# Picking key and value rows from a table on TensorE: one and a half tiles a step with the sums behind the last subtraction, against two tiles a step with x picked

## Chip, cores, metric

The kernel runs on one core of one Trainium2 chip. The metric is the device time of one execution in microseconds (us). The engines are TensorE (PE, with its weight loads as PEld), VectorE (DVE), ScalarE (ACT), GpSimd (POOL) and SyncE (SP), which here only issues transfers.

## What is computed

One layer of a graph network on 6250 nodes of 64 values and 206250 edges, sorted by destination:

```
Qh, Kh, Vh = x @ W.T + b            # [6250, 4 heads, 16]
Ee    = edge_attr @ We.T + be       # [206250, 4, 16]
score = exp(clip((Kh[src] * Qh[dst] / 4 * Ee).sum(-1), -5, 5))
msg   = Vh[src] * score
x     = layernorm(x + segment_sum(msg, dst))
```

`src` is random, `dst` is sorted, so a tile of 128 edges needs 128 scattered rows of K and V, but only a small window of neighbouring rows of Q and of the output.

## The kernel before

**Tiles and steps.** 206250 edges make 1612 tiles of 128; 8 tiles are a group (G), two groups a step. There are 105 steps: 97 of 16 tiles (the steps 0 to 96) and 8 of one group. The order on each engine is the order of the program (the schedule is written by hand); the framework adds the semaphores. Within one PSUM tensor it keeps accesses in order.

**Ahead of the loop** the program writes a table of K and V rows (`kv_tab`, 512 bytes a row) and one of Q rows in three bfloat16 parts to HBM. K and V of the first four groups are computed from gathered rows of x (32 gathers at line 219).

**K and V of a tile** come in one of two ways.

- *Gathered.* `gather_kv` issues one indirect DMA on GpSimd for each tile: 128 rows of `kv_tab` into one of five buffers of a step (`kvs`). `gather(s + 4)` stands in step s, behind `message(s)`.
- *Picked.* In the steps M0 = 4 to LAST = 94 the last two tiles of step s + 2 are not gathered but picked. The table of x is held in SBUF as three bfloat16 parts (`parts`, 50 blocks of 125 nodes, 64 columns a part). `sources` (ScalarE) and `sources_turned` (TensorE, into `from_b` in PSUM) spread the source numbers of a tile over the partitions; `hots` (VectorE, line 470) compares them with the block numbers and makes 25 one-hot matrices in one instruction; `picks` (TensorE, line 480) multiplies them with 25 blocks of the table, 192 columns each. Two `hots` and two `picks` make a tile. `picked`, `picked_turned` and `picked_kv` add the three parts, turn the rows and multiply them with the weights of K and V (lines 487 to 505).

**A step** does, on the critical engines: `queries` (one-hot rows times the window of Q, into PSUM `pq`), `products` (K times Q, times the edge term `pe`), `scores`, `message` (V times score, into `pq`), then three bfloat16 parts of the message (`msg3`): ScalarE copies the first part, TensorE subtracts it in PSUM with a negative identity (`minus`, line 593), ScalarE copies the second, and so on. `sums` (line 601) multiplies one-hot edges with the three parts, 192 columns a tile, into `pa`; `add` puts `pa` onto the accumulator. `spread` and `onehot_rows` make the one-hot rows of the next step: TensorE writes into the one room `pb`, ScalarE squares it out, and a second pass makes the one-hot.

**PSUM.** There are eight banks, and all are taken: `pb`, `pe` and `pq` two each, `pick` (the picked rows) one, `small` one. `small` is shared:

```
small = fixed.tile([P, 4 * P], F32, name="small")
col, from0, from1 = (small[:, i * C:(i + 1) * C].bitcast(BF16) for i in range(3))
score_all = small[:, 3 * C:3 * C + 2 * G * H]
pa = small[:, 4 * C:7 * C].rearrange("p (i c) -> p i c", i=3)
```

**The order around the change.** In step s TensorE gets: spread of the next step's first group, `sums(s - 1)`, the turns, spread of the second group, edges, 25 picks, the turned x rows, edges, and then picks and minus in turn, `queries(s + 1)`, picks. VectorE gets products, picked, scores, `add(s - 1)`, message, two `hots`, the one-hot edges of the next step, two `hots`, and then closing of finished rows and normalising.

Of the kernel before, what the change touches and what calls it, by code (L numbers as in the profile page):

```python
# [14 lines left out]
P = 128  # L15
# [25 lines left out]
TB = 8  # L41
M0 = 4
# [21 lines left out]
LAST = NS - 8 - 3  # L64


def picks_in(s):
    return M0 <= s <= LAST

# [22 lines left out]
def tile_gnn(ctx: ExitStack, tc: tile.TileContext, x, xT, wT, bias, beT, weT, eT, src, dst, dst_rows,  # L92
# [51 lines left out]
    wkv = consts.tile([P, 2, 2 * C], F32, name="wkv")  # L144
    bkv_p = consts.tile([3, G // 2, 2 * C], BF16, name="bkv_p")
    minus_b = consts.tile([P, P], BF16, name="minus_b")
# [26 lines left out]
    with tc.tile_pool(name="nodes", bufs=1) as nodes, \  # L173
# [29 lines left out]

        nc.vector.memset(wkv, 0.0)
# [34 lines left out]
        nc.vector.tensor_scalar(minus_b, ident, -1.0, None, op0=OP.mult)  # L239
# [4 lines left out]
        nc.vector.memset(ones_b, 1.0)  # L244

# [155 lines left out]
    with tc.If(rv == 0) as branch:  # L401

        with tc.tile_pool(name="work", bufs=2) as work, \
# [11 lines left out]
            parts = accp.tile([P, NB, 3, C], BF16, name="parts")  # L415
            nc.vector.memset(parts, 0.0)
            NX = N // NB
            x_v = x.rearrange("(p b) c -> p b c", p=NX)
            n_picks = LAST - M0 + 1
            src_f = accp.tile([P, n_picks, 2], F32, name="src_f")  # L420
            t0 = (M0 + 3) * 2 * G - 2
            for i in range(2):
                nc.vector.tensor_copy(src_f[:, :, i],
                                      src_i[:, t0 + i:t0 + i + 2 * G * (n_picks - 1) + 1:2 * G])
            pick = fixed.tile([P, 4 * P], F32, name="pick")
            rows3 = pick[:, :6 * C].rearrange("p (k i c) -> p k i c", k=2, i=3)
            HOT, FAR, X = {}, {}, {}
# [5 lines left out]
            def table_parts(b):  # L433

                n = min(TB, NB - b)
                raw = work.tile([P, TB, C], F32, name="raw", bufs=1)
                nc.sync.dma_start(raw[:NX, :n], x_v[:, b:b + n, :])
                rest = pick[:NX, :n * C].rearrange("p (b c) -> p b c", b=n)
                nc.scalar.activation(rest, raw[:NX, :n], AF.Copy)
                nc.scalar.activation(parts[:NX, b:b + n, 0], raw[:NX, :n], AF.Copy)  # L440
                return rest

            def table_parts_rest(b, rest):
                n = min(TB, NB - b)
                nc.vector.tensor_sub(rest, rest, parts[:NX, b:b + n, 0])
                nc.scalar.activation(parts[:NX, b:b + n, 1], rest, AF.Copy)
                nc.vector.tensor_sub(parts[:NX, b:b + n, 2], rest, parts[:NX, b:b + n, 1])

            def sources(s, i):

                if picks_in(s):
                    FAR[s, i] = work.tile([P, P], BF16, name="far")
                    nc.scalar.activation(FAR[s, i], row50, AF.Identity,
                                         bias=src_f[:, s - M0, i:i + 1], scale=-1.0)

            def sources_turned(s, i):
                if picks_in(s):
                    nc.tensor.transpose(from_b[i], FAR.pop((s, i)), ident_b)  # L460

            def blocks(h):
                return slice(h * NB // 2, (h + 1) * NB // 2)

            def hots(s, i, h):

                if picks_in(s):
                    HOT[s, i, h] = work.tile([P, NB // 2, P], BF16, name="hot", bufs=4)
                    shape = [P, NB // 2, P // 2, 2]
                    nc.vector.tensor_tensor(  # L470
                        HOT[s, i, h].rearrange("p b (a c) -> p b a c", c=2),
                        pairs(from_b[i])[:, None].to_broadcast(shape),
                        block2[:, blocks(h), None, :].to_broadcast(shape), op=OP.is_equal)

            def picks(s, i, h):
                if picks_in(s):
                    hot = HOT.pop((s, i, h))
                    for k in range(NB // 2):
                        b = h * NB // 2 + k
                        nc.tensor.matmul(rows3[:, i], hot[:, k, :], parts[:, b], start=b == 0,  # L480
                                         stop=b == NB - 1)

            def picked(s):

                if picks_in(s):
                    xp = work.tile([P, 2, C], F32, name="xp")
                    nc.vector.tensor_reduce(xp, rows3.rearrange("p k i c -> p k c i"), axis=AX.X,
                                            op=OP.add)
                    X[s] = xp

            def picked_turned(s):
                if picks_in(s):
                    room = psum.tile([P, G, P], F32, name="pb")
                    nc.tensor.transpose(room[:, 0, :], X[s].rearrange("p k c -> p (k c)"), ident)
                    xe = work.tile([P, P], F32, name="xe")
                    nc.scalar.activation(xe, room[:, 0, :], AF.Copy)
                    X[s] = xe, room[:, 4:6, :]

            def picked_kv(s):
                if picks_in(s):  # L500
                    xe, kv = X.pop(s)
                    nc.tensor.matmul(kv, ones_b, bkv_p[:, :2], start=True, stop=False,
                                     skip_group_check=True)
                    nc.tensor.matmul(kv, xe, wkv, start=False, stop=True, skip_group_check=True)  # L504
                    nc.scalar.activation(kvs[(s + 2) % KVB][:, 2 * G - 2:, :], kv, AF.Copy)

            def gather(s):
                for g in groups_of(s):
                    for j in range(tiles_of(g)):
                        if not picks_in(s - 2) or g == STEPS[s][0] or j < G - 2:  # L510
                            gather_kv(g, j)
# [25 lines left out]

            def onehot_rows_rest(g):
                n = tiles_of(g)
                nc.scalar.activation(TO[g][:, :n, :], TO[g][:, :n, :], AF.Relu, bias=one_p[:3 * W],  # L540
                                     scale=-1.0)
# [11 lines left out]
            def queries(s):  # L553
                PQ[s] = psum.tile([P, 2 * G, C], F32, name="pq")
                for g in groups_of(s):
                    for j in range(tiles_of(g)):

                        nc.tensor.matmul(PQ[s][:, (g - STEPS[s][0]) * G + j, :], TO[g][:, j, :], QW[g],  # L558
                                         start=j == 0, stop=j == tiles_of(g) - 1,
                                         skip_group_check=True)  # L560
# [27 lines left out]
            def minus(s, msg, i):  # L588

                n = tiles_in(s)  # L590
                for lo in range(0, n, G):
                    hi = min(n, lo + G)
                    nc.tensor.matmul(msg[:, lo:hi, :], minus_b, M3[s][:, lo:hi, i, :], start=False,  # L593
                                     stop=True, skip_group_check=True)
                nc.scalar.activation(M3[s][:, :n, i + 1, :], msg[:, :n, :], AF.Copy)  # L595
# [69 lines left out]
            for k, g in enumerate(groups_of(0)):  # L665
                onehot_rows(g, spread(g))
                onehot_rows_rest(g)
                edges(0, k)
            queries(0)
            onehot_edges(0)  # L670
            for s in range(NS):
# [4 lines left out]
                if s + 2 < NS:  # L676
                    for g in groups_of(s + 2):
                        fetch_queries(g)
                nexts = list(groups_of(s + 1)) if more else []
                if more:  # L680
                    onehot_rows(nexts[0], spread(nexts[0]))
                    onehot_rows_rest(nexts[0])
                if s:
                    sums(s - 1)
                sources_turned(s, 1)
                sources_turned(s + 1, 0)
                if nexts[1:]:
                    onehot_rows(nexts[1], spread(nexts[1]))
                making = [b for b in range(s * 2 * TB, (s + 1) * 2 * TB, TB) if b < NB]
                if making:  # L690
                    rest = table_parts(making[0])
                prod = products(s)
                picked(s - 1)
                if more:
                    edges(s + 1, 0)
                picks(s, 0, 0)
                score = scores(s, prod)
                if nexts[1:]:
                    onehot_rows_rest(nexts[1])
# [5 lines left out]
                picked_turned(s - 1)  # L705
                if nexts[1:]:
                    edges(s + 1, 1)
                minus(s, msg, 0)
                hots(s, 1, 0)
                picks(s, 0, 1)  # L710
                minus(s, msg, 1)
                picked_kv(s - 1)
                if not more:

                    close(B - 2)
                    spreads(B - 2)
                hots(s, 1, 1)
                picks(s, 1, 0)
                sources(s + 1, 1)
                sources(s + 2, 0)  # L720
                if more:
# [3 lines left out]
                    queries(s + 1)  # L725
                picks(s, 1, 1)
                hots(s + 1, 0, 0)
                hots(s + 1, 0, 1)
# [19 lines left out]
            sums(NS - 1)  # L748
# [173 lines left out]
```

## Time and profile before

| | |
|---|---|
| time, median of 3 runs | 1808.15 us (1807.94 to 1808.39) |
| the profiled execution | 1808.39 us, its span 1806.6 us |
| busy: PE, PEld, DVE | 1641.5 us (91%), 1370.4 (76%), 1481.7 (82%) |
| busy: ACT, POOL | 912.0 us (50%), 1351.8 (75%) |
| mean granted TensorE clock | 0.95 of full speed |
| transfers | 166.30 MB, mean 92 GB/s |
| gathers of K and V | 1398, and 32 of x |

Busy times count what an engine executes; the issue of an indirect DMA is work of GpSimd and the time between two of them is shown as idle with the releaser "issue". Matmuls overlap in the records (a matmul's time includes its way through the array), so a stream of them is read from start to start. A releaser is inferred from semaphore events; for a wait on several it is the one that came last.

### The profile page before, as it was taken

The numbers are of one execution on the slowest core, as the hardware profiler recorded it, in microseconds if no ns is written. First come the engines' busy times: TensorE is split into PE (matmuls) and PEld (weight loads), VectorE is DVE, ScalarE is ACT, GpSimd is POOL, SyncE is SP. The second block draws the span as 40 slices with busy tenths as digits, with TensorE's granted clock in tenths as the row PEclk, the third lists the DMA queues.
The fourth block names the chain that finished last, engine by engine and source line by source line (L and its number), as shares of the span: only waits on it lengthen the run. The fifth ranks groups of instructions, "written<-read, shape, count | busy, mean of one in ns | idle before, by whom it ended". The sixth has DMA issues, their size and how long they took to land.

```text
span 1806.6 us, 38129 instructions
## 1 busy us (share of the span) xinstructions
PE 1641.5 (91%) x15751; PEld 1370.4 (76%) x15751; DVE 1481.7 (82%) x1695; ACT 912.0 (50%) x1313; POOL 1351.8 (75%) x1442
## 2 busy tenths in 40 slices
PE   8979999999999998999899898989999999999864
PEld 8547888888877777777777787877777778777632
DVE  6459999999988898888888888888988888888554
ACT  4465555555545454544545444455444545445443
POOL 7777777777777777777777777777777777777774
PEclk9968999999999999999999999999999999999855
DMA  8343323333323333332333323323332332332331
GB/s 239 112 120 92 92 80 104 80 101 83 92 79 93 91 84 90 99 81 81 92 91 90 80 79 93 91 79 98 84 92 80 92 91 79 91 91 79 89 79 45
DMA packets 106532, 166.30 MB, mean 92 GB/s; under 512 B 67501, under 2 KB 67822, under 8 KB 106236
## 3 DMA queue, kind: packets, MB, share of 16 engines
q0 software_dynamic: 45760, 92.76, 19.6%
q1 hardware_dynamic: 60204, 70.01, 13.5%
q8 instruction: 125, 2.05, 0.5%
q10 hardware_dynamic: 384, 1.00, 0.3%
q14 instruction: 59, 0.48, 0.1%
HBM read 156.32 MB, written 7.33 MB: 91 GB/s over the span
## 4 chain that ended last, share of the span: by engine, by line
PE 31%; POOL 28%; DVE 19%; issue 14%; DMA 4%; ACT 3%; DVEq 0%; SPq 0%; POOLq 0%; ACTq 0%
POOL kv L391 28%; PE pick L480 15%; DVE hot L470 7%; PE pe L380 4%; DMA kv<-kv_tab,src_i 4%; PE pq L593 2%; DVE prod L565 2%; DVE prod L566 2%; PE small L601 2%; DVE pq L582 2%; DVE small L572 2%; PE pb L518 2%; DVE acc L615 1%; PE pb L504 1%; PE pe L377 1%
## 5 line engine op out<-in xcount | busy, mean ns | idle before, releaser
L391 POOL DMA_INDIRECT kv<-kv_tab,src_i x1398 | 1319.7, 944 | 426.1 <-issue 403.5
L480 PE MATMUL pick<-parts,hot 128*128 128x192 bf16 x9100 | 825.6, 249 | 0.0
L480 PEld LDWEIGHTS <-hot 128*128 128x128 bf16 x9100 | 769.6, 99 | 38.0
L470 DVE TENSOR_TENSOR hot<-small,block 128x3200 bf16<-128x3200 bf16 x364 | 645.9, 1816 | 0.8 <-PE pick L480 0.8
L535 ACT ACTIVATE to<-pb,minus_row 126x1024 bf16<-126x1024 f32 x202 | 222.8, 1103 | 372.7 <-PE pb L518 368.7
L380 PEld LDWEIGHTS pe<-we_sb,et 128*128 128x128 f32 x1612 | 213.2, 206 | 152.9 <-issue 136.8
L595 ACT ACTIVATE msg<-pq 128x1024 bf16<-128x1024 f32 (+2 forms) x210 | 207.8, 990 | 219.7 <-PE pq L593 219.7
L565 DVE TENSOR_TENSOR prod<-kv,pq 128x1024 f32<-128x1024 f32 (+2 forms) x105 | 123.6, 1177 | 191.7 <-DMA kv<-kv_tab,src_i 92.7
L380 PE MATMUL pe<-we_sb,et 128*128 128x128 f32 x1612 | 254.3, 305 | 0.0
L540 ACT ACTIVATE to<-to,one_p 126x1024 bf16<-126x1024 bf16 x202 | 230.6, 1142 | 3.5
L377 PE MATMUL pe<-be_p,ones_b 3*128 3x512 bf16 x202 | 80.0, 396 | 104.8 <-DVE prod L566 104.8
L601 PEld LDWEIGHTS <-of 128*128 128x128 bf16 x1612 | 145.1, 102 | 30.9 <-issue 7.8
L601 PE MATMUL small<-msg,of 128*128 128x192 bf16 x1612 | 161.5, 256 | 0.5 <-ACT msg L595 0.5
L593 PE MATMUL pq<-msg,minus_b 128*128 128x512 bf16 x404 | 128.1, 396 | 30.8 <-ACT msg L585 16.6
L585 ACT ACTIVATE msg<-pq 128x1024 bf16<-128x1024 f32 (+2 forms) x105 | 103.9, 990 | 96.9 <-DVE pq L582 96.9
L572 DVE TENSOR_REDUCE small<-prod 128x64 f32<-128x1024 f32 (+2 forms) x105 | 123.6, 1177 | 13.3 <-PE small L460 7.5
L518 PE MATMUL pb<-key_rows,ident_b 112*128 112x512 bf16 x403 | 127.7, 399 | 2.8 <-ACT to L535 2.8
L566 DVE TENSOR_TENSOR prod<-prod,pe 128x1024 f32<-128x1024 f32 (+2 forms) x105 | 123.6, 1177 | 3.6
L582 DVE TENSOR_TENSOR pq<-kv,small 128x1024 f32<-128x1024 f32 (+2 forms) x105 | 123.5, 1176 | 1.4 <-ACT small L575 1.4
L548 DVE TENSOR_TENSOR of<-small,key 128x2048 bf16<-128x2048 bf16 (+2 forms) x105 | 123.2, 1173 | 0.3
L575 ACT ACTIVATE small<-small 128x64 f32<-128x64 f32 (+2 forms) x105 | 21.7, 207 | 131.0 <-DVE small L574 130.5
L558 PEld LDWEIGHTS <-to 126*128 126x128 bf16 x1612 | 63.5, 101 | 25.1 <-issue 24.9
(128 smaller groups left out, 992.1 us busy)
## 6 DMA issues: line engine op xcount, KB each, us to landing
et<-in_eT SPq DMA_DIRECT2D x100, 512.0 KB
kv<-kv_tab,src_i POOLq DMA_INDIRECT x1398
qw<-q_tab SPq DMA_DIRECT2D x202, 15.8 KB
kv_tab<-kv_sb SPq DMA_DIRECT2D x5, 640.0 KB
q_tab<-q SPq DMA_DIRECT2D x5, 480.0 KB
acc<-in_x SPq DMA_DIRECT2D x48, 32.0 KB
out<-y SPq DMA_DIRECT2D x48, 32.0 KB
raw<-in_x SPq DMA_DIRECT2D x6, 250.0 KB
```

The costliest lines, as they stand in the source:

```text
L380: nc.tensor.matmul(pe[:, 2 * u:2 * u + 2, :], et[:, u, :], we_sb, start=False, stop=u == n // 2 - 1, skip_group_check=True)
L391: nc.gpsimd.indirect_dma_start(out=kv_of(g)[:, j, :], out_offset=None, in_=kv_tab[:, :], in_offset=bass.IndirectOffsetOnAxis(ap=src_i[:, t ...
L470: nc.vector.tensor_tensor(HOT[s, i, h].rearrange("p b (a c) -> p b a c", c=2), pairs(from_b[i])[:, None].to_broadcast(shape), block2[:, bl ...
L480: nc.tensor.matmul(rows3[:, i], hot[:, k, :], parts[:, b], start=b == 0, stop=b == NB - 1)
L518: nc.tensor.matmul(pb[:, b:b + 4, :], ident_b[:NR2, g // 2:g // 2 + 1].to_broadcast([NR2, P]), key_rows[:, g % 2, b * P:(b + 4) * P], star ...
L535: nc.scalar.activation(TO[g][:, :n, :], pb[:3 * W, :n, :], AF.Square, bias=minus_row3[:3 * W])
L540: nc.scalar.activation(TO[g][:, :n, :], TO[g][:, :n, :], AF.Relu, bias=one_p[:3 * W], scale=-1.0)
L565: nc.vector.tensor_mul(prod[:, :n, :], kvs[s % KVB][:, :n, :C], PQ[s][:, :n, :])
L566: nc.vector.tensor_mul(prod[:, :n, :], prod[:, :n, :], PE[s][:, :n, :])
L593: nc.tensor.matmul(msg[:, lo:hi, :], minus_b, M3[s][:, lo:hi, i, :], start=False, stop=True, skip_group_check=True)
L595: nc.scalar.activation(M3[s][:, :n, i + 1, :], msg[:, :n, :], AF.Copy)
L601: nc.tensor.matmul(PA[s], OH[s][:, j, :], M3[s][:, j], start=j == 0, stop=j == n - 1)
```

## The change

The table in SBUF holds K and V themselves (128 columns a part) and is read back from `kv_tab`; so a pick has 384 columns, and the turning of x and the multiplication with the weights are gone. Three tiles are picked in every two steps, from step 9 on (tiles of the steps 11 to 96): 43 x 3 = 129 tiles in place of 182. A step has three units of 25 blocks in place of four. The parts of the message are made by two subtractions on VectorE (`message_rest`, `message_last`) in place of `minus` on TensorE. `queries(s)` moves from the end of step s - 1 to the beginning of step s; both `spread` of the next step stand together behind it; the second pass of `onehot_rows` stands directly behind the first. `sums(s)` stands directly behind `message_last(s)`, ahead of the next `hots`. Core of the diff:

```diff
-TB = 8
-M0 = 4
+TB = 4
+T0 = 2
+M0 = 9
+UNITS = 3
+PICKED = [(s + 2 + d, i) for s in range(M0, NS, 2) for d, i in ((0, 0), (0, 1), (1, 0))
+          if s + 3 < NS and STEPS[s + 3][1] == 2]
...
-            parts = accp.tile([P, NB, 3, C], BF16, name="parts")
-            nc.vector.memset(parts, 0.0)
+            parts = accp.tile([P, NB, 3, 2 * C], BF16, name="parts")
...
-            rows3 = pick[:, :6 * C].rearrange("p (k i c) -> p k i c", k=2, i=3)
+            rows3 = pick[:, :3 * P].rearrange("p (i c) -> p i c", i=3)
...
+            def hots(u):
+                HOT[u] = work.tile([P, NB // 2, P], BF16, name="hot", bufs=3)
+                shape = [P, NB // 2, P // 2, 2]
+                bs = slice(u % 2 * NB // 2, (u % 2 + 1) * NB // 2)
+                nc.vector.tensor_tensor(HOT[u].rearrange("p b (a c) -> p b a c", c=2),
+                                        pairs(from_b[u // 2 % 2])[:, None].to_broadcast(shape),
+                                        block2[:, bs, None, :].to_broadcast(shape), op=OP.is_equal)
+            def picks(u):
+                for i in range(NB // 2):
+                    b = u % 2 * NB // 2 + i
+                    nc.tensor.matmul(rows3, HOT[u][:, i, :], parts[:, b], start=b == 0,
+                                     stop=b == NB - 1)
+            def picked(k):
+                step, back = PICKED[k]
+                nc.vector.tensor_reduce(kvs[step % KVB][:, 2 * G - 1 - back, :],
+                                        rows3.rearrange("p i c -> p c i"), axis=AX.X, op=OP.add)
...
-            def minus(s, msg, i):
...
+            def message_rest(s, msg):
                 n = tiles_in(s)
...
+                nc.vector.tensor_sub(msg[:, :n, :], msg[:, :n, :], M3[s][:, :n, 0, :])
+                nc.scalar.activation(M3[s][:, :n, 1, :], msg[:, :n, :], AF.Copy)
+            def message_last(s, msg):
+                n = tiles_in(s)
+                nc.vector.tensor_sub(M3[s][:, :n, 2, :], msg[:, :n, :], M3[s][:, :n, 1, :])
```

The loop of a step after the change, without the conditions of its ends (`u = (s - M0) * UNITS`; `picked_of(u)` acts for odd u, where a tile is complete):

```
fetch_edges, fetch_queries
queries(s)
for g in nexts:
    onehot_rows(g, spread(g))
for k in turning:
    sources_turned(k, FAR.pop(k))
if making:
    rest = table_parts(making[0])
picks_of(u)
prod = products(s)
edges(s + 1, 0)
picked_of(u)
picks_of(u + 1)
edges(s + 1, 1)
score = scores(s, prod)
add(s - 1)
msg = message(s, score)
gather(s + KVB - 1)
hot_of(u + 2)
picked_of(u + 1)
picks_of(u + 2)
message_rest(s, msg)
keys, onehot_edges(s + 1)
message_last(s, msg)
sums(s)
FAR[...] = sources(...)
hot_of(u + 3)
picked_of(u + 2)
hot_of(u + 4)
close, spreads, roots, scales, norm, table_parts_rest
```

## The prediction

> **What bounds the kernel now.** I read the page's groups first, then the start of every step (L565 opens a step on the Vector engine), one warm step in order of time, the waits, and the granted clock. The groups, with busy time and mean of one, then the idle time before them:
>
> ```profile
> L391 POOL DMA_INDIRECT kv<-kv_tab,src_i x1398 | 1319.7, 944 | 426.1 <-issue 403.5
> L480 PE MATMUL pick<-parts,hot 128*128 128x192 bf16 x9100 | 825.6, 249 | 0.0
> L470 DVE TENSOR_TENSOR hot<-small,block 128x3200 bf16<-128x3200 bf16 x364 | 645.9, 1816 | 0.8 <-PE pick L480 0.8
> ```
>
> GpSimd never stops: 944 ns for a gather and 0.30 us of issue behind it, so 1.2485 us apart. With the 32 gathers of L219 it makes 1430 from 2.94 us on, 1430 x 1.2485 + 2.9 = 1788 us; 18 us remain to the span's end, 1806.6. The starts of L565 agree: steps 6 to 25 take 31.4 us a pair, 15.7 each; from step 26 they take 17.4 to 17.5, which is 14 gathers x 1.2485 = 17.48, and L565 waits for gathered rows. So GpSimd sets the end, and TensorE could do a step in 15.7. That is seen in a warm step:
>
> ```profile
> 270.75 0.60 PE L518 MATMUL pb<-key_rows,ident_b 112*128 112x512 bf16 x2
> 271.18 1.48 PE L601 MATMUL small<-msg,of 128*128 128x192 bf16 x16
> 271.38 1.11 ACT L535 ACTIVATE to<-pb,minus_row 126x1024 bf16<-126x1024 f32 x1 [3.99 <-PE pb L518]
> 272.50 0.28 PE L460 MATMUL small<-ident_b,far 128*128 128x128 bf16 x2
> 272.61 0.60 PE L518 MATMUL pb<-key_rows,ident_b 112*128 112x512 bf16 x2
> 273.14 0.39 PE L377 MATMUL pe<-be_p,ones_b 3*128 3x512 bf16 x1
> 273.46 1.16 PE L380 MATMUL pe<-we_sb,et 128*128 128x128 f32 x8
> 274.45 2.23 PE L480 MATMUL pick<-parts,hot 128*128 128x192 bf16 x25
> 276.51 0.27 PE L494 MATMUL pb<-ident,xp 128*128 128x128 f32 x1
> ```
>
> From start to start: spread 0.43, sums 1.32 (16 of 82.6 ns), two turns 0.11, edges 1.31, 25 picks 2.06. The two spreads share one room in PSUM, so the second starts 1.86 us after the first, behind L535; the sums lie in that gap.
>
> **The gathers.** Picked tiles fall from 182 to 129 (43 x 3), so GpSimd makes 1451 + 32 = 1483 gathers: 53 more, 66 us. Floor: 2.9 + 1483 x 1.2485 + 18 = 1872 of span. In the picking steps it is 14.5 x 1.2485 = 18.1 a step. Nothing hides this; something slower may.
>
> **TensorE's work.** A pick gets 384 columns. Rows at the clock of that step: 64 columns 26.9 ns (L558, 16 in 0.43), 192 columns 82.6, 512 columns 215. The line from 192 to 512 gives 162 (bounds 161 and 165), 25 take 4.06. Per step: 3 x 4.06 = 12.18, edges 2.62, sums 1.32, queries 0.43, spreads 0.86, turns 0.08: 17.5. Gone are one of four batches of 25, the four minus matmuls (0.96) and L494, L502, L504 (0.93).
>
> **The spreads' gap.** Both spreads now stand together behind queries, with nothing between: 1.86 - 0.43 = 1.43 us idle in every step. That makes 18.9.
>
> **The sums ahead of the comparisons.** The sums, turned sources, the scores and the key column all lie in the one PSUM bank of "small". How the program orders that bank is seen in a short step:
>
> ```profile
> 1738.01 1.49 PE L601 MATMUL small<-msg,of 128*128 128x192 bf16 x8
> 1738.12 0.69 DVE L566 TENSOR_TENSOR prod<-prod,pe 128x512 f32<-128x512 f32 x1
> 1739.53 0.69 DVE L572 TENSOR_REDUCE small<-prod 128x32 f32<-128x512 f32 x1 [0.73 <-PE small L601]
> ```
>
> L572 writes columns 192 to 255, L601 columns 256 to 447, yet L572 starts 0.03 us after L601's last matmul. So a comparison (hots, reading small) that follows sums(s) in the program will wait for it on VectorE, and the next turns (writing small) for those comparisons. The trace shows this for a write behind a write; for a read behind a write I take it over. The Trainium skill, "PSUM — Partial Sum Buffer", section "PSUM bank collisions raise a hardware error", says the same of reads and speaks against this change: two engines may not touch one bank and quadrant together, whatever the columns, so semaphores must guard whole banks. By addresses alone the sum would be 1957, by the bank rule 2093.
>
> Time 0 is the start of the sums, which stand behind the third batch of picks on TensorE. VectorE's subtraction is done 1.2 us earlier, then VectorE stands: its next comparison starts at 1.51 (sums 1.48 to the last matmul's end, 0.03). Comparisons start 1.73 apart, the second takes 1.82; every other step a reduction of the pick (0.47, row L487) stands between. So TensorE's turns start at 1.51 + 1.73 + 1.82 + 0.06 = 5.12, or 5.59. TensorE itself got there at 1.32 + 0.43 + 1.86 + 0.43 = 4.04: another 1.08 or 1.55 us idle. Behind the waiting turn are queued the whole 14.8 us of picks and edges, which end the step: 5.12 + 0.06 + 14.8 = 19.98, or 5.59 + 0.11 + 14.8 = 20.50; mean **20.24**. In place of this chain a shorter one (18.9) or a longer one could stand, below.
>
> **VectorE.** Two subtractions of 1024 elements come in; nearest row L582, also 1024 with the output in PSUM, 1.22 us. One comparison of 1.82 goes. Its chain in a step: products 2.5 (L565, L566), scores and exp 1.76 (L572 1.25, L574 0.51), adds 0.66, message 1.13, comparisons 5.2, subtractions and L548 3.5 (the copy on ScalarE, 1.02, hidden behind L548), reductions 0.7, closing 0.75: 16.2. Where it waits for the picks (reduction in the odd step after the first batch at 9.4, in the even one after the second at 15.3) the rest fits: third comparison at 15.25 against 15.94 needed, last subtraction at 19.3 against 20.50. Cover 0.7 and 1.2 us; 0.1 us more on a subtraction costs nothing. ScalarE's second copies move ahead (four of 1.1 in a row until 6.5), exp is due at 9.2 or later. I cost these edits at nothing, as I do the queues that sums is moved past: ScalarE's far (0.4 each) and SyncE's loads and stores of closing and norm, none of which reads the sums. POOL's gather stays behind message. The larger table (13 loads of 256 KB for 7 of 250) is made in steps 2 to 8, where a step of before with two parts takes 16.0 (steps 0 to 2), mostly waits between ScalarE and VectorE.
>
> **The clock.** TensorE falls to half for 3.41 us when the 3.41 us before held little work, on a fixed grid of such stretches. The columns are the stretch, then busy times, then the clock:
>
> ```profile
> 912.14:915.55 3.41, 1.95 (x16) 1.42 (x15) 3.34 (x5) 1.78 (x2) 2.56 (x3) 1.00 0.22 55
> 915.55:918.97 3.42, 3.40 (x33) 2.86 (x32) 3.14 (x5) 2.31 (x4) 2.51 (x4) 1.00 0.15 41
> 929.21:932.62 3.41, 1.13 (x8) 0.43 (x6) 3.03 (x4) 2.07 (x2) 2.50 (x4) 0.99 0.47 156
> 932.62:936.03 3.41, 3.41 (x21) 3.25 (x21) 3.10 (x6) 1.26 (x2) 2.56 (x3) 0.50 0.25 65
> ```
>
> Between steps 5 and 95 all ten warm stretches with up to 1.61 us of work led to half clock, none with 1.86 or more. A low costs 3.41 / 2 = 1.7 us. The new step has 2.2 to 5.6 us with only 0.6 of work, so a stretch that covers it goes low: about 2 of 3.41 us of phase. But 20.24 is 0.24 short of six stretches (20.48): the thin part slides by 0.24 a step into a stretch, one low moves it 1.7 - 0.24 further, out again, and some seven steps pass until the next. The mean is then six stretches, **20.48** (bounds: no low 20.24, all low 21.95). The Trainium skill, "TensorE: Matmul & The Clock Gate", section "What's actually happening", has half clock after an idle window of about 3.4 us. No window here is quite idle, so the page alone would give 20.24 and 2072; the rows above show that 1.1 us of work did not keep the clock.
>
> **The sum**, on the profiled execution. First L565 at 84.4, as before; steps 0 and 1 14.5 each (VectorE's chain 10.8 with the copies bare, cold sums and queries 3.7), 2 to 7 16.0, step 8 17: 226. Then 86 steps (9 to 94) x 20.48 = 1761: 1987. Steps 95 and 96 without picks 14 each, seven short ones as before (1792.73 - 1727.77 = 65): 2080; tail 13.9 as before, less some tenths: span 2093, less 2 as step 94 compares nothing more: 2091. Around the span the profiled execution has 1808.39 - 1806.6 = 1.8, and it lies 0.2 above the median: **2093 us**.
>
> **Rivals.**
> - The comparisons don't wait for the sums (ordering by column). Then only the 1.43 gap is left: 18.9 x 86 = 1625, so 1957. For it: no read of small is seen waiting in this trace. Against: L572. 0.12.
> - Lows in most steps: if the natural step is over 20.48 the thin part slides the other way and meets two lows in a row. Between 21 and 21.95 a step: 2140 to 2219. For it: only 0.24 away. 0.17.
> - GpSimd bounds: TensorE under 18.1 a step, if the gaps close: 1872 + 1.8 = 1874. Against: 17.5 of work leaves 0.6 for gaps of 2.5. 0.03.
> - Not slower: gathers come faster as picking thins. It decides from 1430 / 1483 x 1.2485 = 1.204 us a gather, 1808 there and 1802 at 1.20. Against: the spacing is 1.2485 at 10 us with VectorE idle and at 900 with it full; TensorE would also have to do its step in 17.4. 0.02.
>
> **How the numbers follow.** Forecast case 0.66, alone 2070 to 2120. The range must take in the first rival, the only large one below, and the lower part of the second: 1950 to 2160, leaving out some 0.15. Faster or slower by 0.2% (3.6 us) is about what a measurement can tell from no change: faster 0.01, same 0.01, slower 0.98.
>
> **What would show it.** Right: comparisons (hots) idle some 2.7 us a step with the sums as releaser, over 200 us in all; TensorE's spread waiting 1.4 us for ScalarE; step starts 20 to 20.6 apart with a longer one each seven or so; GpSimd with idle time for buffers. Wrong: no idle time before hots (first rival); a mean clock under 0.93 in the middle (second); GpSimd without gaps and 18.1 a step (third).

## The result and the profile after

The changed kernel takes 2123.5 us (median of 4 runs, 2119.4 to 2135.3) against 1808.1: 1.1755 times the time before, 95% interval 1.1705 to 1.1804. The forecast was 2093, with a range of 1950 to 2160. The profiled execution is the longest of the four: 2135.3 us, span 2133.4, mean clock 0.943; the reading below is of this one.

The groups of the changed kernel, with busy time and mean of one, then the idle time of the engine before them and its releaser:

```profile
L388 POOL DMA_INDIRECT kv<-kv_tab,src_i x1451 | 1369.3, 944 | 673.1 <-issue 409.3
L465 PE MATMUL pick<-parts,hot 128*128 128x384 bf16 x6450 | 1111.8, 331 | 0.4 <-DVE hot L458 0.4
L458 DVE TENSOR_TENSOR hot<-small,block 128x3200 bf16<-128x3200 bf16 x258 | 465.7, 1819 | 238.8 <-PE small L562 208.2
L484 PE MATMUL pb<-key_rows,ident_b 112*128 112x512 bf16 x403 | 130.0, 406 | 135.9 <-ACT to L501 135.9
```

GpSimd, which set the end before, now has 673 us of idle time before its gathers, of which only 409 is issue. The comparisons (L458) had 0.8 us of idle time before them in the kernel before; here it is 238.8. The sums (L562) end 208.2 of it; the other 30.6 is put down to the queries (L520), which stand right behind the sums on TensorE. The waits say what stands behind what; the columns are the total, how often, and the longest, in us:

```profile
POOL kv L388 <- DVE pq L543: 254.6, 79, 11.3
DVE hot L458 <- PE small L562: 208.2, 75, 2.9
PE pb L484 <- ACT to L501: 135.9, 96, 6.0
PE small L451 <- DVE hot L458: 96.9, 82, 1.4
```

VectorE waits for the sums, TensorE's turns (L451) wait for VectorE's comparisons, and GpSimd waits for a buffer that the message (L543) frees. So the order is reversed: the gathers now follow the step. The shares of the chain that ended last agree:

```profile
PE 65%; DVE 14%; POOL 9%; issue 7%; ACT 3%; DMA 1%; DVEq 0%; SPq 0%; ACTq 0%; POOLq 0%
```

One step in order of time, from one set of sums to the next, and the beginning of the step behind it (start, duration, engine, and in brackets the idle time ahead with its releaser). Only the lines that the reading needs are shown:

```profile
903.42 1.23 DVE L556 TENSOR_TENSOR msg<-pq,msg 128x1024 bf16<-128x1024 f32 x1
906.03 1.48 PE L562 MATMUL small<-msg,of 128*128 128x192 bf16 x16
907.55 1.83 DVE L458 TENSOR_TENSOR hot<-small,block 128x3200 bf16<-128x3200 bf16 x1 [2.90 <-PE small L562]
907.82 0.60 PE L484 MATMUL pb<-key_rows,ident_b 112*128 112x512 bf16 x2
909.62 0.59 PE L484 MATMUL pb<-key_rows,ident_b 112*128 112x512 bf16 x2 [1.20 <-ACT to L501]
911.62 0.27 PE L451 MATMUL small<-ident_b,far 128*128 128x128 bf16 x2 [1.42 <-DVE hot L458]
911.73 4.23 PE L465 MATMUL pick<-parts,hot 128*128 128x384 bf16 x25
915.89 0.39 PE L374 MATMUL pe<-be_p,ones_b 3*128 3x512 bf16 x1
917.20 4.23 PE L465 MATMUL pick<-parts,hot 128*128 128x384 bf16 x25
922.67 4.23 PE L465 MATMUL pick<-parts,hot 128*128 128x384 bf16 x25
...
926.73 1.48 PE L562 MATMUL small<-msg,of 128*128 128x192 bf16 x16
928.25 3.55 DVE L458 TENSOR_TENSOR hot<-small,block 128x3200 bf16<-128x3200 bf16 x2 [2.78 <-PE small L562]
931.86 0.22 PE L451 MATMUL small<-ident_b,far 128*128 128x128 bf16 x1 [0.95 <-DVE hot L458]
```

VectorE's last subtraction ends at 904.65. Its next comparison starts 2.90 us later, 1.52 after the first sum and as the last sum ends. It reads the turned sources; the sums write other columns of the same bank. The turns start 5.59 after the sums in the one step and 5.13 in the other, and behind them 25 + 25 + 25 picks and the edges follow without a gap. The sums of successive steps that no lower clock disturbs lie 20.70 and 20.18 apart in turn, 20.44 in the mean. The longer kind has two turns and a reduction between its comparisons, the shorter one turn.

### The profile page after: what moved, and what is told of

It is laid out like the page before. It is cut to its first block, busy times and chain, and to the rows that moved or that the text cites. A ratio compares the mean times of both kernels' runs of the same rounds, so it can differ in the third digit from the quotient of the medians.

```text
span 2133.4 us, 30970 instructions
## 1 busy us (share of the span) xinstructions
PE 1792.6 (84%) x12280; PEld 1163.3 (55%) x12280; DVE 1570.8 (74%) x1848; ACT 769.9 (36%) x991; POOL 1401.3 (66%) x1495
## 3 DMA queue, kind: packets, MB, share of 16 engines
q8 instruction: 98, 1.61, 0.3%
## 4 chain that ended last, share of the span: by engine, by line
PE 65%; DVE 14%; POOL 9%; issue 7%; ACT 3%; DMA 1%; DVEq 0%; SPq 0%; ACTq 0%; POOLq 0%
PE pick L465 44%; DVE hot L458 10%; POOL kv L388 9%; PE pe L377 8%; PE small L562 6%; PE pe L374 2%; DVE kv L470 1%; PE small L451 1%; ACT to L501 1%; PE ps L336 1%; PE pv L368 1%; ACT to L503 1%; DMA kv<-kv_tab,src_i 1%; DVE pq L543 1%; DVE pq L551 1%
## 5 line engine op out<-in xcount | busy, mean ns | idle before, releaser
L388 POOL DMA_INDIRECT kv<-kv_tab,src_i x1451 | 1369.3, 944 | 673.1 <-issue 409.3
L465 PE MATMUL pick<-parts,hot 128*128 128x384 bf16 x6450 | 1111.8, 331 | 0.4 <-DVE hot L458 0.4
L465 PEld LDWEIGHTS <-hot 128*128 128x128 bf16 x6450 | 634.3, 99 | 452.4 <-issue 73.9
L458 DVE TENSOR_TENSOR hot<-small,block 128x3200 bf16<-128x3200 bf16 x258 | 465.7, 1819 | 238.8 <-PE small L562 208.2
L562 PE MATMUL small<-msg,of 128*128 128x192 bf16 x1612 | 168.4, 264 | 76.6 <-DVE msg L556 72.1
L552 ACT ACTIVATE msg<-pq 128x1024 bf16<-128x1024 f32 (+2 forms) x105 | 103.8, 989 | 274.5 <-DVE pq L551 274.5
L562 PEld LDWEIGHTS <-of 128*128 128x128 bf16 x1612 | 150.4, 105 | 94.2 <-issue 81.1
L546 ACT ACTIVATE msg<-pq 128x1024 bf16<-128x1024 f32 (+2 forms) x105 | 103.8, 989 | 198.1 <-DVE pq L543 198.1
L470 DVE TENSOR_REDUCE kv<-pick 128x128 f32<-128x384 f32 x129 | 71.5, 554 | 133.2 <-PE pick L465 133.2
L551 DVE TENSOR_TENSOR pq<-pq,msg 128x1024 f32<-128x1024 f32 (+2 forms) x105 | 124.0, 1181 | 16.6 <-ACT msg L546 16.6
L484 PEld LDWEIGHTS <-ident_b 112*128 112x128 bf16 x403 | 33.6, 101 | 177.3 <-issue 166.4
L556 DVE TENSOR_TENSOR msg<-pq,msg 128x1024 bf16<-128x1024 f32 (+2 forms) x105 | 124.0, 1181 | 1.4 <-ACT msg L552 0.8
L543 DVE TENSOR_TENSOR pq<-kv,small 128x1024 f32<-128x1024 f32 (+2 forms) x105 | 123.5, 1176 | 1.5 <-ACT small L536 1.5
```

What stands on the lines that cost most here:

```text
L388: nc.gpsimd.indirect_dma_start(out=kv_of(g)[:, j, :], out_offset=None, in_=kv_tab[:, :], in_offset=bass.IndirectOffsetOnAxis(ap=src_i[:, t ...
L458: nc.vector.tensor_tensor(HOT[u].rearrange("p b (a c) -> p b a c", c=2), pairs(from_b[u // 2 % 2])[:, None].to_broadcast(shape), block2[:, ...
L465: nc.tensor.matmul(rows3, HOT[u][:, i, :], parts[:, b], start=b == 0, stop=b == NB - 1)
L484: nc.tensor.matmul(pb[:, b:b + 4, :], ident_b[:NR2, g // 2:g // 2 + 1].to_broadcast([NR2, P]), key_rows[:, g % 2, b * P:(b + 4) * P], star ...
L543: nc.vector.tensor_mul(msg[:, :n, :].rearrange("p g (h d) -> p g h d", h=H), kvs[s % KVB][:, :n, C:].rearrange("p g (h d) -> p g h d", h=H ...
L551: nc.vector.tensor_sub(msg[:, :n, :], msg[:, :n, :], M3[s][:, :n, 0, :])
```

## Experiments

The first eight ran on chips on which the kernel before takes 1808.4; the last four on a chip of the same kind where it takes 3014.6. "Step" is the mean distance of the 86 picking steps (from the products of step 9 to those of step 95); it is 20.75 in the changed kernel.

**Who waits for whom, the other way round.** `sums(s)` moves behind the step's last comparison in the program.

```diff
                 message_last(s, msg)
-                sums(s)
                 FAR[...] = sources(...)
                 hot_of(u + 3)
                 picked_of(u + 2)
                 hot_of(u + 4)
+                sums(s)
```

> sums(s) stands behind the step's last comparison in the program; the order on TensorE and on VectorE stays as in the changed kernel, only who waits for whom in the bank of 'small' turns round. Bank order (my theory): the sums now wait for two comparisons, done 2.3 or 2.8 us after the place where they stood, and everything behind them waits too: turns at 6.4 or 6.8 us in place of 5.1 or 5.6, 1.2 us more in each of 86 steps: about 2225 us, up to 2310 if the longer idle time brings more half clock. Order by columns (rival): nothing in the order of the engines changed, so the time of the changed kernel, 2123, within 1%.

Measured: 2317.7 us (1.2827, 1.2807 to 1.2846), step 22.83. VectorE's and TensorE's own order is the same as in the changed kernel. Only which of two instructions on different engines comes first in the program has changed, and the wait has turned round: no idle time before the comparisons, and the sums wait for them.

```profile
L458 DVE TENSOR_TENSOR hot<-small,block 128x3200 bf16<-128x3200 bf16 x258 | 464.8, 1816 | 0.0
```

```profile
PE small L562 <- DVE hot L458: 205.2, 86, 7.1
```

Columns of a read and a write that don't overlap are ordered all the same; the rival by column, which made this the same time as the changed kernel, falls. `small` is one tensor that fills one bank, so no run here tells an order by bank from an order by tensor. The time lies 8 us above the expected range: TensorE now stands 2.1 or 2.4 us ahead of the sums besides the 1.2 in the second spread, and 76 stretches of the half clock (3.41 us each) fall in these steps against 14.

**The sums in the spreads' gap.** `sums(s - 1)` stands between the two spreads of step s.

```diff
-                for g in nexts:
+                for i, g in enumerate(nexts):
                     onehot_rows(g, spread(g))
+                    if i == 0 and s:
+                        sums(s - 1)
...
                 message_last(s, msg)
-                sums(s)
```

> sums(s-1) stands between the two spreads of step s, as in the kernel before; the rest is the changed kernel. Bank order: comparisons no longer wait for the sums, but the sums wait for the second comparison (2.3 or 2.8 us); behind them spread, turns and picks: picks start at 4.2 or 4.7 in place of 5.2 or 5.7: 1.0 us less in 86 steps, about 2040 us (2010 to 2070, the clock may shift it). Rival (only the 1.43 us gap between the spreads counted, comparisons are free): 17.9 us of TensorE a step, so GpSimd with 18.1 bounds: 1880 to 1910 us.

Measured: 2001.7 us (1.1066, 1.1049 to 1.1083), step 19.48. Of the orders tried that keep the bank shared it is the best, and it lies 8 us below the expected range. The comparisons don't wait at all, the sums wait for them in every second step:

```profile
PE small L562 <- DVE hot L458: 76.3, 47, 2.2
```

Taken with the first experiment, the place of the sums alone moves the time over 316 us, from 2002 to 2318. The change's place lies in between.

**One spread apart.** The second spread and its one-hot stand behind the first picks, as a gap on TensorE would then be filled by picks.

```diff
-                for g in nexts:
+                for g in nexts[:1]:
                     onehot_rows(g, spread(g))
...
                 picks_of(u)
+                for g in nexts[1:]:
+                    onehot_rows(g, spread(g))
```

> The second spread and its two ScalarE passes stand behind the first batch of picks; nothing else moves. Theory: the gap of 1.43 us lies within the wait of the turns for the comparisons, so closing it wins nothing, and the second spread (0.43 us) now adds to TensorE behind the wait: 86 x 0.43 = 37 us more, 2160 us (2130 to 2200 with the clock). Rival (each gap of TensorE counts by itself, as 17.5 + 1.43 + the rest): 86 x 1.43 = 123 us less, 2000 us.

Measured: 2201.9 us (1.2189, 1.2170 to 1.2207), step 21.51. The second spread and its 1.2 us of idle time go from there, and the turns wait 1.8 us a step longer for the comparisons (96.9 us before in all):

```profile
PE small L451 <- DVE hot L458: 252.2, 85, 3.2
```

So the spreads' gap costs nothing in the changed kernel: the turn is reached earlier and starts no earlier. The 78 us on top (67 between the two profiled executions) are, as far as they can be told apart, two things. The shortest steps, from sums to sums, are 20.61 and 21.13 in place of 20.18 and 20.70: the spread's 0.43 moved from inside the wait to behind it, 86 x 0.43 = 37. And 36 stretches at half clock stand there in place of 14: 22 at 1.8 (next experiment) are 40. The time lies 2 us above the expected range.

**More work, less time.** The queries of a step are made three times more between its two spreads (48 more matmuls of 64 columns in each of 86 steps).

```diff
-                PQ[s] = psum.tile([P, 2 * G, C], F32, name="pq")
+                if s not in PQ:
+                    PQ[s] = psum.tile([P, 2 * G, C], F32, name="pq")
...
                     onehot_rows(g, spread(g))
+                    if i == 0 and M0 <= s <= 94:
+                        for _ in range(3):
+                            queries(s)
```

> queries(s) is repeated three times between the two spreads of the steps 9 to 94: the same 16 matmuls of 64 columns into the same places, 3 x 0.43 = 1.29 us of work in a gap of 1.43. Theory: the thin stretch then holds about 1.9 us of work, no 3.41 us stretch falls to half clock in the picking steps, and the mean step goes from 20.75 to 20.44: 2100 to 2110 us, with less spread between runs. Rival A (the low clock costs nothing here): 2123, same. Rival B (the work adds itself): 86 x 1.29 = 111 us more, 2235.

Measured: 2114.5 us (five runs, 2114.0 to 2115.1; 1.1692, 1.1676 to 1.1708), step 20.54, with natural steps of 20.2 and 20.7 as before. 135 us more in records of these matmuls (70.5 before, 205.5 here) make the kernel 9 us faster. The stretches at half clock in the picking steps fall from 14 to 4, and those four lie behind two stalls of another kind (below); the runs lie within 1.1 us of each other instead of 16. The gain is small (the intervals just touch, 1.1705 and 1.1708), but all five runs lie below all four of the changed kernel; the time is 4 us above the expected range, as the two stalls stay. Ten stretches for 0.21 x 86 = 18 us of the two profiled executions: 1.8 us each, near the 1.7 of the forecast.

**VectorE's cover.** The last subtraction is done twice, and in another kernel three times.

```diff
                 message_last(s, msg)
+                message_last(s, msg)        # the second kernel: two of these
                 sums(s)
```

> message_last is done twice (the same subtraction into the same place), 1.14 to 1.22 us more on VectorE between the last ScalarE copy and the sums. Theory: it has a cover of 1.3 us (VectorE done at 925.47, sums begin at 926.73 in the profile), so it costs nothing: 2123 within 1% (2110 to 2145, the clock's noise). Rival (VectorE's chain is on the path): 86 x 1.2 = 100 us more, 2225.

> message_last three times, 2.3 to 2.4 us more. Theory: the cover of 1.3 us is gone and 1.0 to 1.1 us a step comes out: 86 to 95 us more, about 2215, and more still (up to 2290) if the longer idle time ahead of the sums brings half clock. Rival (VectorE has far more room than that, since it then stands 2.8 us for the sums): 2123, same.

Measured: 2155.7 us (1.1911, 1.1887 to 1.1934) and 2367.0 (1.3084, 1.3062 to 1.3105). In the first the undisturbed picking steps keep their length (20.19 and 20.76 against 20.18 and 20.70), so a whole subtraction of 1.2 us is just covered. The time is 11 us above the expected range, though: the cost lies in the 19 steps without picks, which the expectation had left out (the products of step 9 at 253 instead of 242, the end at 115 instead of 107), and in 8 more stretches at half clock. In the second the cover is gone and the sums wait for the subtraction:

```profile
PE small L562 <- DVE msg L556: 216.1, 104, 9.4
```

The step is 23.0, with 62 stretches at half clock, and the time is 77 us above the expected range. Of the 231 us between this profiled execution and the changed kernel's some 108 are the longer undisturbed steps (21.38 and 22.03, 1.26 more in the mean), 86 the 48 more stretches at 1.8, and 37 the steps without picks. One more subtraction cost 32 us, the next 211: the cover is about 1.2 us, as the forecast had it for the last subtraction (1.38 ahead of the first sums shown above, 1.26 ahead of the next).

**The gathers.** Of each of the steps 11 to 96 the first gather is left out, so that 86 fewer are issued.

```diff
+                        if 11 <= s <= 96 and g == STEPS[s][0] and j == 0:
+                            continue
                         if (s, 2 * G - 1 - (g - STEPS[s][0]) * G - j) not in PICKED:
```

> The first gather of each of the steps 11 to 96 is left out (86 gathers; that tile computes with old rows). Theory: GpSimd is ahead and waits for free buffers in the picking steps, so nothing changes: 2123 within 1% (2105 to 2140). Rival (GpSimd's gathers set the end, as in the kernel before): 86 x 1.2485 = 107 us less, 2016.

Measured: 2124.2 us (1.1747, 1.1725 to 1.1769), the changed kernel's time. GpSimd has less to do and waits longer for the buffers (254.6 us after, here 343.2):

```profile
L388 POOL DMA_INDIRECT kv<-kv_tab,src_i x1365 | 1291.4, 946 | 741.3 <-issue 379.3 <-DVE pq L545 343.2 <-DMA kv<-kv_tab,src_i 10.1
```

**The picks' columns.** A pick takes 256 columns in place of 384.

```diff
-                    nc.tensor.matmul(rows3, HOT[u][:, i, :], parts[:, b], start=b == 0,
+                    nc.tensor.matmul(rows3[:, :2], HOT[u][:, i, :], parts[:, b, :2], start=b == 0,
...
-                                        rows3.rearrange("p i c -> p c i"), axis=AX.X, op=OP.add)
+                                        rows3[:, :2].rearrange("p i c -> p c i"), axis=AX.X, op=OP.add)
```

> The third bfloat16 part of the table is left out of the picks: 256 columns in place of 384, same number of matmuls and comparisons. Theory: 25 matmuls take 25 x (256/2.4 + 2.5) = 2.73 us in place of 4.06, 4.0 us less TensorE a step: 20.4 - 4.0 = 16.4, so others bound: VectorE with its wait for the sums (16.2 + 1.6 = 17.8) or GpSimd (18.1): 1880 to 1930 us, GpSimd without waits for buffers. Rival (the columns are hidden, the order of waits sets the step): less than 1% faster.

Measured: 1932.1 us (1.0670, 1.0647 to 1.0692), step 18.44, just above the expected range, with 40 stretches at half clock. The picks are on the path: 191 us go with a third of them. At this length GpSimd hardly waits for buffers any more (36 us after 255); what is left is the 0.30 of issue between its gathers:

```profile
POOL kv L388 <- issue: 423.5, 1389, 0.5
POOL kv L388 <- DVE pq L543: 36.3, 16, 8.5
```

**The bank taken away.** ScalarE copies the turned sources to SBUF, and the comparisons read the copy; the order is the changed kernel's.

```diff
+            FROM = {}
...
                 nc.tensor.transpose(from_b[k % 2], far, ident_b)
+                FROM[k] = work.tile([P, P], BF16, name="from", bufs=3)
+                nc.scalar.copy(FROM[k], from_b[k % 2])
...
-                                        pairs(from_b[u // 2 % 2])[:, None].to_broadcast(shape),
+                                        pairs(FROM[u // 2])[:, None].to_broadcast(shape),
```

> ScalarE copies the turned sources (128 columns) out of PSUM behind each turn, and the comparisons read the copy; nothing else is moved, the sums still stand ahead of the comparisons. Bank theory: the comparisons no longer touch the bank of the sums, so their wait (2.9 a step) and the turns' wait for them (1.1 to 1.6) go. What is left is the work of TensorE (17.5, and 0.2 for the two batches that are followed by edges, 4.16 in place of 4.06) and the spreads' gap of 1.43: 19.1 a step in place of 20.75; with the start to step 9 (242), 86 x 19.1 = 1643, the end (106) and 2 around it 1993 us; 1960 to 2040, as the scores may now wait for the copy (ScalarE reaches it some 7 us into the step) and as lows of the clock may stay at the roots. Rival, the comparisons wait for the sums for another reason (their place in the program, or the buffers of the one-hot matrices): about 2123.

Measured: 3145.9 us, 1.0424 times the 3014.6 of before on that chip (1.0393 to 1.0454). The time can't be set beside the expected one: on that chip engines stand 10 to 25 us at a time, in about every other step, and the profile shows nothing that they wait for ("remote", or "issue"). Most single operations take as long as elsewhere. But between these stalls whole steps are undisturbed, and there the theories can be told apart:

```profile
L462 DVE TENSOR_TENSOR hot<-from,block 128x3200 bf16<-128x3200 bf16 x258 | 465.3, 1818 | 0.0
```

That is the group; one such step in order of time (only the lines that the reading needs):

```profile
1516.49 3.55 DVE L462 TENSOR_TENSOR hot<-from,block 128x3200 bf16<-128x3200 bf16 x2
1518.67 1.48 PE L566 MATMUL small<-msg,of 128*128 128x192 bf16 x16
1519.99 0.63 PE L524 MATMUL pq<-qw,to 126*128 126x64 bf16 x16
1522.26 0.59 PE L488 MATMUL pb<-key_rows,ident_b 112*128 112x512 bf16 x2 [1.20 <-ACT to L505]
1522.69 0.22 PE L453 MATMUL small<-ident_b,far 128*128 128x128 bf16 x1
1522.75 4.22 PE L469 MATMUL pick<-parts,hot 128*128 128x384 bf16 x25
1525.47 0.25 ACT L455 COPY from<-small 128x128 bf16<-128x128 bf16 x1
1537.74 1.48 PE L566 MATMUL small<-msg,of 128*128 128x192 bf16 x16
```

The comparisons now start ahead of the sums and never wait (0.0 against 238.8 us); the turn stands right behind the second spread, 4.02 after the sums in place of 5.13. From sums to sums it is 19.07 us in 36 of the 86 picking steps, to 0.01, where the expectation had 19.1. The program's order was not touched; only the room that the comparisons read has changed. That the shared room of `small` is the cause of VectorE's wait is so shown.

But all 36 are steps with one turn. In a step with two turns the second turn, a write into `small`, waits for ScalarE's copy of the first, a read of other columns of `small` that stands behind four passes of the one-hot rows on ScalarE:

```profile
PE small L453 <- ACT from L455: 108.8, 38, 2.9
```

```profile
1537.74 1.48 PE L566 MATMUL small<-msg,of 128*128 128x192 bf16 x16
1541.76 0.22 PE L453 MATMUL small<-ident_b,far 128*128 128x128 bf16 x1
1544.55 0.24 ACT L455 COPY from<-small 128x128 bf16<-128x128 bf16 x1
1544.84 0.27 PE L453 MATMUL small<-ident_b,far 128*128 128x128 bf16 x1 [2.86 <-ACT from L455]
```

The picks then start 7.16 after the sums in place of 4.08. The expectation had left this wait out. No step of this kind ran without a stall here, so its length is an estimate, 19.07 + 3.08 = 22.15; in the run `e11_copied_early` below, with the same copy, the two kinds measured 17.75 and 20.84. The mean is then 20.6 a step, and with 242 to step 9 and 106 at the end 86 x 20.6 makes some 2120 us on the other chips, also an estimate: what the copy takes from VectorE's wait it gives back on TensorE, by the same order within `small`.

**Both at once.** The copy, and the sums between the spreads (the two diffs above together).

> As the run with the copied sources, and the sums of step s - 1 stand between the two spreads of step s. Bank theory: both waits of the changed kernel are gone at once and the sums fill the spreads' gap, so TensorE could do a step in 17.8, less than the 18.1 of 14.5 gathers: GpSimd sets the step. 18.1 to 18.6 a step, with the start of 233 that the run with the sums between had: 233 + 86 x 18.4 = 1582 + 106 + 2 = 1923 us; 1885 to 1965. Rival, the turns' wait in the run with the sums between (2001.7) was not the bank: 2000 again.

Measured: 2865.2 us on that chip, 0.9492 of before there (0.9443 to 0.9540). The shortest steps, 17 of them, have 17.75 us from sums to sums, against the 17.8 expected of TensorE. Again these are steps with one turn; with two, the second turn waits 2.87 for ScalarE's copy. With 20.84 for those (next run) the mean is 19.3, over the 18.1 of the gathers, and 233 + 86 x 19.3 + 106 + 2 makes some 2000 us elsewhere, an estimate and no better than the 2002 of the same order without the copy. The expectation that both waits go at once and GpSimd sets the step is so not borne out, and this chip, where all steps together take 27.7 in the mean, can't measure it. This version and its variant below are the only ones that beat the kernel before, and only on this chip, where the stalls make up some 30% of the step (27.7 against 19.3). With 1483 gathers the floor elsewhere stays the forecast's 1874, above 1808.

**Two small stalls.** `raw` gets two buffers and is loaded ahead of the step's closing, and the square roots of the first two batches stand behind the next step's message; once on the version just shown, once on the one with more queries.

```diff
...
+                for b in making:
+                    table_load(b)
                 if making:
                     rest = table_parts(making[0])
...
                 msg = message(s, score)
+                if late:
+                    roots(*late)
...
```

> As the run before it, and two small things: the raw rows of the table are loaded ahead of the step's other transfers into two buffers, so that no second load stands behind a closing's on SyncE's queue (three steps of 2 to 3 us in the changed kernel), and the square roots of the first two batches of rows stand behind the next step's message, where no square of the next one-hot rows waits behind them (2 to 4 us each, and a low of the clock behind them). Expected: 10 to 16 less than the run before it, about 1910; 1875 to 1950; the floor of 1483 gathers stays 1874, so that it does not come under the 1808 of before. Rival, GpSimd bounds that run already, so that these two are hidden: the same as that run, within 3.

> The changed kernel's order with three more queries between the spreads (2114.5), and the raw rows loaded early and the square roots late as in the run before. Expected: three steps with a closing lose 2.8 each (8), the two stalls at the roots go with their four lows (about 10): 2096 us, 2085 to 2106, and lengths of 18.8 to 19.2 and 21.7 to 22.1 in all other steps as before. So the distance of the changed kernel to the sum of the forecast would be: natural step of 20.44 in place of 20.24, and these two. Rival, the start and the two long pairs of steps have another cause: 2114.

Measured: 2889.8 us (0.9569, 0.9513 to 0.9624) and 3167.4 (1.0508, 1.0486 to 1.0530), both on the slow chip. Neither tells anything on its question, which is about 10 to 20 us: the first lies 25 above the version that it was to improve, and the two intervals overlap.

## Why the prediction was right

**The mechanism held, step by step.** Its chain for one step was: sums 1.51 to the first comparison, turns at 5.12 or 5.59, picks and edges 14.8, so 19.98 and 20.50. Measured: 1.52, 5.13 and 5.59, and 20.2 and 20.7. The bank rule was taken over from one short step of before, where a write waited behind a write (0.73); that a read waits behind a write was open, at 0.12 for the rival. The experiment with the sums behind the comparisons and that with the copy decide it: the order follows the program within `small`, in both directions, and goes when the reader leaves it. Two of the forecast's signs are there with their sizes: 238.8 us before the comparisons, 2.8 a step (over 200, 2.7), and 1.2 in each second spread (1.4 by the forecast's account, which reads from start to start). The sign in the step starts is there in part: they are 20.18 and 20.70 apart from sums to sums, but some 19 and 22 in turn from products to products, and the lows come in nine groups, not one in seven steps.

**The terms that cost nothing.** One subtraction more is indeed covered, and 86 fewer gathers change nothing. The spreads' gap of 1.43 is on the path in the forecast's shorter chain and hidden in the longer; the spread set apart agrees.

**What was mis-sized.** By the profiled execution the forecast is 42 us short, 16 of it up to step 9, 23 in the 86 steps and 3 at the end:

- *Up to step 9: 226, measured 242.* Steps 2 to 8 were put at 16.0, by steps of before with two parts. Here the three with a closing of rows take 18.7 to 19.8 and two without 16.6. In the trace the second load of raw rows stands on SyncE's queue behind the closing's load, and ScalarE's first pass over it waits 1.6 to 2.7 us for the transfer. The forecast went past this queue with "none of which reads the sums", which is true and not the point. That this is the cause was read from the trace; the runs that were to show it fell on the slow chip.
- *The step: 20.24 natural, measured 20.44.* A batch of 25 picks takes 4.06 where sums follow (922.67 to 926.73 above), as forecast, and 4.16 where edges follow (911.73 to 915.89): 0.1 twice a step, 17 us in all.
- *The clock: a mean of 20.48, measured 20.75.* The forecast had the natural step slide along the grid of stretches, with one low in seven steps. At 20.44 a pair of steps is 40.88, only 0.08 short of twelve stretches of 3.413, so that, it seems, the thin part of the step stays long where no low meets it, and lows come in clusters: 14 stretches. So the sliding that the forecast worked out did not happen; that its price is near (26 us in the 86 steps, some of it the stalls below, against 21) is luck. The forecast's rule for a low held one way: ahead of each group of lows TensorE had at most 1.62 us of work in the 3.41 (it had said 1.61). The other way it did not: the stretch 776.73:780.14 with 1.48 us of work left the full clock behind it, and with the sums behind the comparisons 582.10:585.50 with 1.45 did. So 1.6 is no fixed bound. Four of the groups in the changed kernel, the columns being the stretch ahead of the low, the busy times with counts of PE, PEld, DVE, ACT and POOL, the granted clock, the share of the DMA engines and GB/s:

```profile
445.64:449.05 3.41, 1.62 (x22) 0.82 (x20) 3.25 (x3) 2.31 (x3) 2.50 (x4) 0.99 0.23 55
469.53:472.94 3.41, 1.33 (x15) 0.53 (x12) 3.41 (x3) 2.60 (x3) 2.49 (x4) 0.99 0.15 40
780.14:783.56 3.42, 0.00 (x0) 0.00 (x0) 2.93 (x8) 0.58 (x2) 2.51 (x4) 0.99 0.21 52
824.52:827.93 3.41, 1.39 (x17) 0.59 (x14) 3.41 (x3) 2.54 (x3) 2.50 (x4) 0.99 0.23 58
```

  Of nine such groups two follow a stretch without any work; the other seven follow 1.3 to 1.6 us of it. The Trainium skill's "What's actually happening" ("TensorE: Matmul & The Clock Gate"), which has the half clock after an idle window, covers only the two, so here the measurement decides. Two of the groups, four stretches, belong to steps 35 and 68. There the square root of the norm sits on ScalarE ahead of the next squares and waits for VectorE:

```profile
ACT rstd L606 <- DVE rstd L605: 17.8, 4, 7.9
```

  and TensorE's second spread waits 6.0 and 5.3 us for ScalarE and then works at half clock. From the sums ahead of them to the next these two steps take 26.9 and 26.7 us. Of the 26 us by which the 86 steps exceed 86 x 20.44, the run with more queries takes 18 away and leaves these two.
- *The end, from the products of step 95 on: 106, less 2 for step 94, measured 107.*

So the likeliest case was the right one; its size was right in the chain and 1.5% low by the median, for the queue (by the trace alone), the batches ahead of edges and the lows.

## What to carry to other kernels

Look for every PSUM room that several engines share (here one tensor that fills one bank), and put a moved writer in the program where no reader or writer of it on another engine is next: here one line's place was worth 316 us, and columns that don't overlap did not help. A copy out of the room is a reader too: here the next turn waited 2.9 us for it in every second step. Work out the new chain per step on both engines from start to start, since two waits (VectorE for TensorE, then TensorE for VectorE) come out of one such ordering, and a gap beside them may be free. Then count TensorE's idle time in a step: here the clock made it cost a second time.

## What the runs showed of the hardware that was not expected

- **TensorE's idle time is paid twice.** With 3.3 to 3.6 us of it in a step (the sums behind the comparisons, in two pieces) 76 stretches of the picking steps went to half clock, with 2.7 or 3.2 (one spread apart, in one piece) 36, with 2.2 to 2.6 (the changed kernel, in two pieces) 14, and with 0.9 or 1.4 (queries in the gap) 4, behind stalls of another kind. Both of the first came out above their expected range.
- **Useless work can pay.** 48 matmuls of 64 columns in each step's gap made the kernel 9 us faster (2114.5 against 2123.5, with intervals that just touch), and its runs spread over 1 us instead of 16.
- **A kernel's time can differ by two thirds between chips of a kind.** The kernel before took 1808 us on the first ones and 3015 on the last, a single chip. In the traces of the copied versions there most gathers (87% and 84%) take the same 944 to 947 ns and a comparison the same 1.82 us, but engines stood for 10 to 25 us without a releaser. What holds them was not found.
